# Statistics, norm and weight sums of the first batch, and the last three outputs, put on other engines in a two-layer attention kernel

## The chip, the cores and the metric

The kernel runs on one core of a Trainium2 chip. The metric is the device time of one execution in microseconds (us); less is better. PE stands for TensorE, PEld for its weight loads, DVE for VectorE, ACT for ScalarE, POOL for GpSimd and SP for SyncE, which issues most DMAs.

## The reference

The input `x` holds 8 images of 32x32 tokens with 512 channels, in fp32. Two layers follow each other. Each normalises `x` over groups of 16 channels (no scale, no shift), applies attention and adds the result to `x`:

```
x = x + proj(attention_16_heads_of_32(gn(x) @ w_qkv)) + b_proj
x = x + attention_4_heads_of_128(gn(x) @ Wq, Wk, Wv, with position logits) @ Wo
```

where `gn(v) = (v - mean) / sqrt(var + 1e-5)` over the 1024 tokens and the 16 channels of a group. The second layer's scores get two logits per pair of positions, from the queries and two small embeddings.

## The kernel before

All work is in fp32, channels on the partitions: one image is a block of 128 partitions x 4 chunks of channels x 1024 tokens. Products of 512x512 weights are formed by a seven-product scheme: the image's two halves and the weights' quarters are first combined into sums, then seven smaller products replace eight. The sums of the image ("forms", `forming`, L436) are four additions of 128x1024 on VectorE; the sums of the weights (`Matrix.add_up`, L177) are four subtractions of 128x512 a matrix, once for the whole run, stored to DRAM (L179) for the later batches.

A pass over the batches weaves three things on TensorE: the first layer's attention of batch b, what is left of batch b - 1 (projection, second layer), and the loading and projections of batch b + 1. The order of the instructions on each queue is decided when the program is built: the functions are generators that yield after each piece, `woven` and `side_by_side` pull from them in turn, and a scheduler then places the instructions. `tc.issue_after(x)` keeps an instruction behind `x` in that order.

What the change touches is the start and the end, where there is only one batch.

The start is `load_first`, then the sums of WV0, WQ0 and WK0 (value, query and key weights of the first layer), then `before_first`. `load_first` fetches the image's rows in eight DMAs on SP and ACT (L1175) and the three weights on SP (L163). TensorE turns the rows into channels, 32 blocks of 128x128 (L1193): the first 512 tokens (h = 0) into one PSUM tile of four banks, the second 512 (h = 1) into four tiles of a bank each. ScalarE copies each bank to SBUF (`x0T`, L1201), and VectorE takes the statistics of each bank (L1203). TensorE runs eight matmuls whose result is not used (L1207). VectorE aggregates (L318) and averages over groups (L329 to L354), GpSimd takes the power -1/2 (L363), VectorE normalises four chunks of 128x1024 (L367, into `xn`) and forms the sums (L436). SP stores the four chunks of `x0T` for the later residual (`put_away`, L275) and then fetches the next image in blocks (`xs`, L293).

Then come the weight sums: of WV0 two on GpSimd and two on VectorE, of WQ0 and WK0 four each on VectorE, placed behind the last form (`last_form`). `before_first` makes half of the values, queries and keys with `seven`: products x, y and z of 32 matmuls or fewer into three banks; between them VectorE adds snapshots `a` (L487) and `b` (L495) out of the bank y, and TensorE must not add the next product into y before VectorE has read it. `begun[0]` is the latest `a`.

The end is `after_last`: the output projection of the last batch, units u = 0 and u = 1, in `in_two_parts` with `five_alone` for the last five products. As each quarter of a unit's result is added to the residual (L672), `put_out` turns it in 32x32 blocks on VectorE (L1380) and sends it out in four DMAs of 64 KB, on SP and ACT in turn (L1385); each is made of pieces of 128 bytes, 32 channels of one token. Unit 1's quarters come in the order (0,0), which is sent long before the end, then (0,1), (1,1) and (1,0), the last of which waits for the last product.

Of the kernel before, what the change touches and what calls it, by code (L numbers as in the profile page):

```python
# [9 lines left out]
F32 = mybir.dt.float32  # L10
# [17 lines left out]
def quick_path(  # L28
# [123 lines left out]
    class Matrix:  # L152
# [12 lines left out]
        def add_up(self, engines, store, keep=False):  # L165

            t = self.t
            whole = t[:, : CC // 2, :].rearrange("p a (b n) -> p (a b) n", n=NB)
            sums = t[:, CC // 2 :, :].rearrange("p a (b c n) -> p (a b) c n", c=HC, n=HN)
            b11, b12, b21, b22 = [quarter(whole, i) for i in (11, 12, 21, 22)]  # L170
            for i, (x, y) in enumerate(
                [(b12, b11), (b22, sums[:, 0]), (b22, b12), (b21, sums[:, 1])]
            ):

                engine = engines[i]
                with tc.issue_after(last_form[0].ins) if engine is nc.vector else nullcontext():
                    engine.tensor_tensor(sums[:, i], x, y, op=ALU.subtract)  # L177
            d = dram.tile([P, 4, HC, HN], F32, tag="sums", name=f"ws_{self.name}", bufs=8)
            store.dma_start(d, sums)  # L179
            self.t = d  # L180
            self.kept = (whole, sums) if keep else None

        def factor(self, i):

# [138 lines left out]
    def group_norm(st, xT, name, after=None, behind=None, out=None, apart=False):  # L323

        mv = st.pop("mv")

        def averages(out, src, tag):
            total = small.tile([P, 2], F32, tag=f"total{tag}", name=f"total{tag}_{name}")
            nc.vector.tensor_reduce(  # L329
                total, src.rearrange("p (g k) -> p g k", k=GROUP_CHANNELS), axis=AX.X, op=ALU.add  # L330
            )
            nc.vector.tensor_scalar(
                out.rearrange("p (g k) -> p g k", k=GROUP_CHANNELS),
                total.unsqueeze(2).to_broadcast([P, 2, GROUP_CHANNELS]),
                1.0 / GROUP_CHANNELS,
                None,
                op0=ALU.mult,
            )

        turned = small.tile([P, 32], F32, tag="turned", name=f"turned_{name}")  # L340

        with tc.issue_after(after().ins) if after is not None else nullcontext():
            nc.vector.transpose(turned, mv)
        avg = small.tile([P, 2, 32], F32, tag="avg", name=f"avg_{name}")
        averages(avg[:, 0, :], turned, 0)

        nc.vector.tensor_sub(turned, turned, avg[:, 0, :])
        nc.vector.tensor_mul(turned, turned, turned)
        averages(avg[:, 1, :], turned, 1)
        back = small.tile([P, 2, 32], F32, tag="back", name=f"back_{name}")  # L350
        nc.vector.transpose(back.rearrange("p a c -> p (a c)"), avg.rearrange("p a c -> p (a c)"))
        mean = back[:, 0, :CC]
        var = small.tile([P, CC], F32, tag="var", name=f"var_{name}")
        nc.vector.scalar_tensor_tensor(  # L354
            var, back[:, 0, CC : 2 * CC], GN_EPS, back[:, 1, :CC], op0=ALU.add, op1=ALU.add
        )
        if apart:

            mean = small.tile([P, CC], F32, tag="mean0", name=f"mean_{name}")
            nc.vector.tensor_copy(mean, back[:, 0, :CC])  # L360
            yield 0
        rstd = small.tile([P, CC], F32, tag="rstd0" if apart else "rstd", name=f"rstd_{name}")
        nc.gpsimd.tensor_tensor(rstd, var, neg_half, op=ALU.pow)  # L363
        yield 0
        for cc in range(CC):
            with tc.issue_after(behind().ins) if behind is not None else nullcontext():
                nc.vector.tensor_scalar(  # L367
                    xT[cc] if out is None else out[cc],
                    xT[cc],
                    mean[:, cc : cc + 1],  # L370
                    rstd[:, cc : cc + 1],
                    op0=ALU.subtract,
                    op1=ALU.mult,
                )
            if cc % 2 or apart:
                yield 0
# [793 lines left out]
    def load_first(st):  # L1170

        rows = block("x_rows", [P, NT, C])
        for t in range(NT):
            queue = nc.scalar if t % 2 else nc.sync
            queue.dma_start(rows[:, t, :], xf[0, t * P : (t + 1) * P, :])  # L1175
        for m in (WV0, WQ0, WK0):
            m.fetch(nc.sync)
        x = block("x0T_0")
        xT = chunks(x)
        looks = mem.tile([P, NB], F32, tag="row", name="looks", bufs=3)  # L1180
        looks = looks[:, : CC * NH * 6].rearrange("p (c h s) -> p c h s", c=CC, s=6)
        looks = [looks[:, cc] for cc in range(CC)]
        looked, copied = [None], [None]
        for h in range(NH):
            if h == 0:
                whole = wide_tile("turned_0")
                banks = [whole[:, cc, :] for cc in range(CC)]
            else:
                banks = [bank(f"turned_1_{cc}") for cc in range(CC - 1)]
                banks.append(psum.tile([P, NB], F32, tag="acc", name="turned_1", bufs=1))  # L1190
            for t in range(NT // NH):
                for cc in range(CC):
                    nc.tensor.transpose(  # L1193
                        banks[cc][:, t * P : (t + 1) * P],
                        rows[:, h * (NT // NH) + t, cc * P : (cc + 1) * P],
                        ident,
                    )
            for cc in (0, 2, 1, 3):
                part = xT[cc][:, h * NB : (h + 1) * NB]
                with tc.issue_after(copied[0].ins) if copied[0] is not None else nullcontext():  # L1200
                    copied[0] = nc.scalar.copy(part, banks[cc])  # L1201
                with tc.issue_after(looked[0].ins) if looked[0] is not None else nullcontext():
                    looked[0] = nc.vector.bn_stats(looks[cc][:, h, :], banks[cc])  # L1203

        idle = wide_tile("idle")
        for t in range(NT):
            nc.tensor.matmul(idle[:, t % CC, :], ident, rows[:, t, :], start=True, stop=True)  # L1207
        st["mv"] = mvs[0]
        mvs.reverse()
        for cc in (0, 2, 1, 3):  # L1210
            aggregate(st, looks[cc], cc)
        st["kept"] = put_away(xT, "0_0")

        xn = block("xn0_0")
        run(group_norm(st, xT, "0_0", out=chunks(xn)))
        st["xn"] = forms(xn, "xn0_0")

# [156 lines left out]
    def put_out(b, st, xT, u):  # L1374
        def put(n, h):
            m = n * HC + u
            ot = mem.tile([P, NB], F32, tag="row", name=f"ot_{b}_{m}_{h}", bufs=3)
            late = b == B - 2
            with tc.issue_after(added[0].ins) if late else nullcontext():
                nc.vector.transpose(ot, xT[m][:, h * NB : (h + 1) * NB])  # L1380
            ot = ot.rearrange("p (t i) -> p t i", i=32)
            for a in range(P // 32):

                queue = nc.scalar if b == B - 1 and a % 2 else nc.sync
                queue.dma_start(  # L1385
                    by_blocks(of[b, h * NB : (h + 1) * NB, :], m * P + 32 * a),
                    ot[32 * a : 32 * a + 32],
                )

        def put_later(n, h):  # L1390
            st.setdefault("late", []).append(lambda: put(n, h))

        return put_later if b == B - 2 else put

    def late_output(st):

# [4 lines left out]
    def after_last(b, st):  # L1401

        x = st["ao"]
        xT = fetch(st["kept"], block(f"x2T_{b}"))
        sinks = [Onto(halves(xT, u), then=put_out(b, st, xT, u)) for u in range(2)]
        run(
            in_two_parts(
                x, WO, sinks, f"wo_{b}", behind=(None, None, None, lambda: begun[0]), in_turn=True,
                first=ends.pop(),
            )  # L1410
        )

    def woven(main, side, start, gap, places=(0,)):

# [78 lines left out]
    ends = []  # L1493
    load_first(states[0])
    WV0.add_up([nc.gpsimd] * 2 + [nc.vector] * 2, nc.gpsimd, keep=True)
    WQ0.add_up([nc.vector] * 4, nc.gpsimd, keep=True)
    fill_fold()
    stream = Stream(plan)

    def key_sums():  # L1500
        WK0.add_up([nc.vector] * 4, nc.gpsimd, keep=True)
        yield 0

    def other_sums():
        for m in (WP, WQ1, WK1, WV1, WO):
# [1 line left out]
            m.add_up([nc.gpsimd] * 4, nc.gpsimd)  # L1507
            yield 0

    run(woven(before_first(states[0]), key_sums(), 3, 1))  # L1510
    for b in range(B + 1):
        rest, total = [], 0
        s = [None] * 2 + states + [None] * 2
# [577 lines left out]
```

## Time and profile before

| What | Value |
|---|---|
| Time, median of 3 runs | 3664.14 us (3663.9 to 3664.3) |
| The profiled execution | 3663.89 us |
| Its span in the profile | 3662.1 us |
| TensorE busy | 3633.3 us (99%) |
| VectorE busy | 2557.9 us (70%) |
| ScalarE busy | 1999.3 us (55%) |
| GpSimd busy | 1298.3 us (35%) |
| Granted TensorE clock, mean | 0.999 |

The span runs from the first to the last record of the program; 1.8 us of the profiled execution's time lie outside it. A line of the timeline has the begin in us from the span's start, the duration, the engine, the line of the kernel, the operation, the tile written and those read, the shape and the count; in brackets stands how long the engine was idle before and what ended that. Equal instructions that follow each other are merged. A line by stretches has the stretch, its length, the busy time of each engine with the number of instructions, the TensorE clock, the busy share of the 16 DMA engines and their GB/s. Ends of matmuls are modelled.

### The profile page before, as it was taken

The numbers are of one execution on the slowest core, as the hardware profiler recorded it, in microseconds if no ns is written. First come the engines' busy times: TensorE is split into PE (matmuls) and PEld (weight loads), VectorE is DVE, ScalarE is ACT, GpSimd is POOL, SyncE is SP. The second block draws the span as 40 slices with busy tenths as digits, with TensorE's granted clock in tenths as the row PEclk, the third lists the DMA queues.
The fourth block names the chain that finished last, engine by engine and source line by source line (L and its number), as shares of the span: only waits on it lengthen the run. The fifth ranks groups of instructions, "written<-read, shape, count | busy, mean of one in ns | idle before, by whom it ended". The sixth has DMA issues, their size and how long they took to land.

```text
span 3662.1 us, 81197 instructions
## 1 busy us (share of the span) xinstructions
PE 3633.3 (99%) x33996; PEld 1243.4 (34%) x34002; DVE 2557.9 (70%) x2911; ACT 1999.3 (55%) x2281; POOL 1298.3 (35%) x833
## 2 busy tenths in 40 slices
PE   8999999999999999999999999999999999999998
PEld 4222244232433234332343323433234232323343
DVE  6788657786677856679566795767856678566545
ACT  2555666546654466544665446654566545656254
POOL 1343155131541316313173131822328122165254
PEclk9999999999999999999999999999999999999999
DMA  6233164342644326343363443533336133324376
GB/s 191 67 113 105 43 172 137 83 124 66 184 128 128 90 64 192 116 129 92 79 192 103 122 95 102 183 92 118 83 98 206 53 99 79 98 93 155 97 203 146
DMA packets 582069, 431.98 MB, mean 118 GB/s; under 512 B 280608, under 2 KB 472384, under 8 KB 580672
## 3 DMA queue, kind: packets, MB, share of 16 engines
q1 hardware_dynamic: 570064, 410.92, 39.9%
q0 software_dynamic: 2608, 13.70, 1.0%
q8 instruction: 270, 4.42, 0.5%
q10 hardware_dynamic: 9024, 2.10, 0.3%
q14 instruction: 103, 0.84, 0.1%
HBM read 334.30 MB, written 92.27 MB: 116 GB/s over the span
## 4 chain that ended last, share of the span: by engine, by line
PE 95%; DVE 3%; ACT 1%; issue 1%; POOL 0%; DMA 0%; SPq 0%; DVEq 0%; ACTq 0%; POOLq 0%
PE ps L791 15%; PE acc L817 13%; PE ps L1010 12%; PE acc L1024 12%; PE y_v L397 4%; PE y_q L397 4%; PE y_k L397 4%; PE z_q L397 3%; PE x_v L397 3%; PE z_v L397 3%; PE x_k L397 3%; PE x_q L397 3%; PE z_k L397 3%; PE y_wp L397 2%; PE y_wo L397 2%; PE sums L839 2%
## 5 line engine op out<-in xcount | busy, mean ns | idle before, releaser
L806 ACT ACTIVATE e_room<-ps 128x2048 f32<-128x2048 f32 x512 | 961.9, 1879 | 745.7 <-PE ps L791 725.2
L829 DVE TENSOR_TENSOR e_room<-e_room 128x2048 f32<-128x2048 f32 x448 | 1078.4, 2407 | 398.7 <-ACT e_room L806 397.0
L960 POOL TENSOR_TENSOR pos<-pos,columns 128x512 f32<-128x512 f32 x448 | 645.9, 1459 | 194.3 <-DMA pos<-pr 186.5
L791 PE MATMUL ps<-q,k 32*64 32x512 f32 x8192 | 592.5, 613 | 1.0 <-ACT e_room L806 1.0
L817 PE MATMUL acc<-e_room,v 128*32 128x512 f32 x4096 | 546.8, 604 | 0.1
L1010 PE MATMUL ps<-q,k 128*128 128x512 f32 x1024 | 530.2, 600 | 0.5 <-ACT ps L969 0.5
L1024 PE MATMUL acc<-e,v 128*128 128x512 f32 x1024 | 523.0, 593 | 0.0
L1013 ACT ACTIVATE e<-ps 128x512 f32<-128x512 f32 x512 | 305.8, 597 | 323.9 <-PE ps L1010 315.1
L1040 DVE TENSOR_TENSOR es<-es,e 128x512 f32<-128x512 f32 x384 | 277.8, 723 | 211.8 <-ACT e L1013 208.2
L772 POOL TENSOR_TENSOR q<-q,su 128x512 f32<-128x512 f32 x64 | 104.9, 1639 | 539.2 <-DVE su L768 515.4
L1024 PEld LDWEIGHTS acc<-e,v 128*128 128x128 f32 x1024 | 193.3, 190 | 247.6 <-issue 132.5
L969 ACT COPY ps<-pos 128x512 f32<-128x512 f32 x448 | 264.7, 592 | 10.4 <-PE ps L982 7.5
L1010 PEld LDWEIGHTS ps<-q,k 128*128 128x128 f32 x1024 | 187.3, 190 | 231.0 <-issue 207.2
L791 PEld LDWEIGHTS ps<-q,k 32*64 32x64 f32 x8192 | 122.9, 129 | 391.2 <-issue 212.1
L817 PEld LDWEIGHTS acc<-e_room,v 128*32 128x32 f32 x4096 | 81.4, 108 | 411.5 <-issue 363.6
L656 POOL TENSOR_TENSOR k<-b_k,p_k 128x512 f32<-128x512 f32 x32 | 50.1, 1566 | 479.1 <-ACT p_k L501 474.7
L656 POOL TENSOR_TENSOR q<-b_q,p_q 128x512 f32<-128x512 f32 x32 | 60.6, 1895 | 357.2 <-ACT p_q L501 342.7
L656 POOL TENSOR_TENSOR v<-b_v,p_v 128x512 f32<-128x512 f32 x32 | 50.6, 1582 | 258.8 <-ACT p_v L501 255.9
L889 ACT COPY pos<-pp 32x512 f32<-32x512 f32 x128 | 104.3, 815 | 29.2 <-PE pp L880 27.9
L1038 DVE TENSOR_TENSOR es<-e,e 128x512 f32<-128x512 f32 x64 | 64.9, 1014 | 70.4 <-ACT e L1013 70.2
L733 DVE STREAM_TRANSPOSE tu<-su 128x512 f32<-128x512 f32 x64 | 45.2, 706 | 82.4 <-ACT su L731 82.3
L397 PE MATMUL y_q<-f_xn,w_q 128*32 128x512 f32 x768 | 91.3, 593 | 1.3 <-DVE a_q L487 1.3
(233 smaller groups left out, 4564.5 us busy)
## 6 DMA issues: line engine op xcount, KB each, us to landing
pos<-pr SPq DMA_DIRECT2D x448, 256.0 KB, 3.3
w_qkv<-ws_qkv SPq DMA_DIRECT2D x168, 128.0 KB, 2.6
x1T<-d SPq DMA_DIRECT2D x32, 512.0 KB, 5.4
d<-x1T SPq DMA_DIRECT2D x32, 512.0 KB, 3.6
pc<-pos SPq DMA_DIRECT2D x32, 512.0 KB, 6.5
pr<-pos SPq DMA_DIRECT2D x32, 512.0 KB, 7.7
columns<-pc SPq DMA_DIRECT2D x64, 256.0 KB, 4.0
x2T<-d SPq DMA_DIRECT2D x32, 512.0 KB, 6.6
```

The costliest lines, as they stand in the source:

```text
L397: ins = nc.tensor.matmul(out[columns, :], weights[:, columns], moving, start=start, stop=stop, skip_group_check=open_sum,)
L656: nc.gpsimd.tensor_tensor(self.dst[1][1], s(b), s(p7), op=ALU.add)
L791: nc.tensor.matmul(ps[some, r, :], k[m][rows, j * P + 64 * i : j * P + 64 * i + 64], q[m][rows, h * NB : (h + 1) * NB], start=True, stop=True,
L806: exps[0] = nc.scalar.activation(e, ps, AF.Exp, scale=D0 ** -0.5)
L817: nc.tensor.matmul(acc[r * D0 : (r + 1) * D0, :], v[:, j, c0 : c0 + D0], e[:, r, :], start=(j == blocks[0]), stop=(j == blocks[-1]),)
L829: summed[0] = nc.vector.tensor_add(state["esum"], state["esum"], e)
L960: nc.gpsimd.tensor_tensor(self.rows[i], self.rows[i], self.columns[i // NT], op=ALU.add)
L969: self.copied = nc.scalar.copy(ps, rows)
L1010: scored[0] = nc.tensor.matmul(ps, k[h][:, keys], q[:, h, queries], start=False, stop=True, skip_group_check=True)
L1013: exps[0] = nc.scalar.activation(e, ps, AF.Exp, scale=1.0 / math.sqrt(D1))
L1024: nc.tensor.matmul(acc, v[:, j, h * D1 : (h + 1) * D1], e, start=(j == 0), stop=(j == NT - 1),)
L1040: added[0] = nc.vector.tensor_add(state["esum"], state["esum"], e)
```

## The change

There are five edits.

1. The statistics of the first half (h = 0) read ScalarE's copy in SBUF instead of the PSUM bank; those of the second half still read the banks.
2. In the first batch's norm, chunks 2 and 3 go to ScalarE as an Identity activation with scale rstd and bias -mean x rstd. The bias is a new 128x4 VectorE operation, kept in the unused end of the tile that holds the statistics. Chunks 0 and 1 stay on VectorE.
3. The sums of WQ0 and WK0 are no longer issued in a row behind the last form: each is placed behind the latest `a` (`begun`), and `first_sums` yields after each one, woven into `before_first` from its second piece on. WV0's sums stay.
4. In the built program this places WQ0's four sums and the first of WK0 between a_v and b_v, two of WK0 behind b_v and the last behind a_q; WK0's store on GpSimd comes behind the addition of a part of v. Nine matmuls of x_v's second product stand ahead of y_v's first, and one of x_q's inside z_v's last two.
5. The last three outputs of the last batch are kept back and turned by TensorE in four 128x128 transposes each, behind the last product; ScalarE copies the first two, VectorE the third, out of PSUM, and each goes out in one DMA of 256 KB, in pieces of 512 bytes: the first and third on SP, the second on ACT.

All other instructions stand in the same order on every queue. The blocks of SBUF that k of batch 0 and x0T of batch 1 use have changed places.

```diff
+        def add_apart(self, store):
+
+            whole, sums = self.keep()
+            b11, b12, b21, b22 = [quarter(whole, i) for i in (11, 12, 21, 22)]
+            pairs = [(b12, b11), (b22, sums[:, 0]), (b22, b12), (b21, sums[:, 1])]
+            for i in (0, 1, 2, 3):
+                with tc.issue_after(begun[0].ins):
+                    nc.vector.tensor_tensor(sums[:, i], *pairs[i], op=ALU.subtract)
+                if i == 3:
+                    d = dram.tile([P, 4, HC, HN], F32, tag="sums", name=f"ws_{self.name}", bufs=8)
+                    store.dma_start(d, sums)
+                    self.t = d
+                yield 0
...
-        for cc in range(CC):
+        if out is not None:
+
+            offset = st.pop("spare")
+            nc.vector.scalar_tensor_tensor(offset, mean, -1.0, rstd, op0=ALU.mult, op1=ALU.mult)
+            for cc in range(CC // 2, CC):
+                nc.scalar.activation(
+                    out[cc], xT[cc], AF.Identity, scale=rstd[:, cc : cc + 1], bias=offset[:, cc : cc + 1]
+                )
+        for cc in range(CC if out is None else CC // 2):
...
-                    looked[0] = nc.vector.bn_stats(looks[cc][:, h, :], banks[cc])
+
+                    looked[0] = nc.vector.bn_stats(looks[cc][:, h, :], banks[cc] if h else part)
...
-        return put_later if b == B - 2 else put
+        def put_last(n, h):
+            if (n, h) == (0, 0) or u == 0:
+                return put(n, h)
+            st.setdefault("late", []).append((n, h, xT[n * HC + u]))
+
+        return put_later if b == B - 2 else put_last if b == B - 1 else put
+
+    def last_output(b, st):
+
+        for i, (n, h, x) in enumerate(st.pop("late")):
+            m = n * HC + 1
+            name = f"last_{m}_{h}"
+            if i == 0:
+                turned = psum.tile([P, NB], F32, tag="acc", name=name, bufs=1)
+            else:
+                turned = bank(name)
+            for t in range(NB // P):
+                at = slice(t * P, (t + 1) * P)
+                nc.tensor.transpose(turned[:, at], x[:, h * NB : (h + 1) * NB][:, at], ident)
+            ot = mem.tile([P, NB], F32, tag="row", name=f"ot_{name}", bufs=3)
+            if i == 2:
+                nc.vector.tensor_copy(ot, turned)
+            else:
+                nc.scalar.copy(ot, turned)
+            queue = nc.scalar if i == 1 else nc.sync
+            queue.dma_start(
+                of[b, h * NB : (h + 1) * NB, m * P : (m + 1) * P].rearrange("(t p) c -> p t c", p=P),
+                ot.rearrange("p (t c) -> p t c", c=P),
+            )
...
-    WQ0.add_up([nc.vector] * 4, nc.gpsimd, keep=True)
     fill_fold()
     stream = Stream(plan)
 
-    def key_sums():
-        WK0.add_up([nc.vector] * 4, nc.gpsimd, keep=True)
-        yield 0
+    def first_sums():
+        for m in (WQ0, WK0):
+            yield from m.add_apart(nc.gpsimd)
...
-    run(woven(before_first(states[0]), key_sums(), 3, 1))
+    WQ0.keep()
+    run(woven(before_first(states[0]), first_sums(), 1, 1))
```

More of the change, by code (lines that the diff above doesn't have):

```diff
@@ L181, in add_up, with keep @@
             self.kept = (whole, sums) if keep else None
+        def keep(self):
+            whole = self.t[:, : CC // 2, :].rearrange("p a (b n) -> p (a b) n", n=NB)
+            sums = self.t[:, CC // 2 :, :].rearrange("p a (b c n) -> p (a b) c n", c=HC, n=HN)
+            self.kept = (whole, sums)
+            return whole, sums
+        def add_apart(self, store):
[10 more added lines that the diff above has]
+                yield 0
         def factor(self, i):
@@ L1179, in load_first @@
         xT = chunks(x)
-        looks = mem.tile([P, NB], F32, tag="row", name="looks", bufs=3)
-        looks = looks[:, : CC * NH * 6].rearrange("p (c h s) -> p c h s", c=CC, s=6)
+        room = mem.tile([P, NB], F32, tag="row", name="looks", bufs=3)
+        looks = room[:, : CC * NH * 6].rearrange("p (c h s) -> p c h s", c=CC, s=6)
+        st["spare"] = room[:, NB - CC :]
         looks = [looks[:, cc] for cc in range(CC)]
@@ L1411, in after_last @@
         )
+        last_output(b, st)
     def woven(main, side, start, gap, places=(0,)):
```

## The prediction

> **What bounds the kernel now.** I read the page first, then the busy time by stage, then the timelines of the two ends.
>
> ```profile
> span 3662.1 us, 81197 instructions
> PE 3633.3 (99%) x33996; PEld 1243.4 (34%) x34002; DVE 2557.9 (70%) x2911; ACT 1999.3 (55%) x2281; POOL 1298.3 (35%) x833
> ```
>
> TensorE is idle for 3662.1 - 3633.3 = 28.8 us in all. Where, the busy time by stage says (stretch, its length, then busy time of PE, PEld, DVE, ACT, POOL, then clock, DMA share, GB/s):
>
> ```profile
> 0.00:22.40 22.40, 14.72 (x50) 9.54 (x51) 10.67 (x29) 5.59 (x9) 6.77 (x17) 0.92 0.95 337
> 22.40:37.63 15.23, 12.88 (x226) 7.90 (x229) 12.91 (x18) 1.76 (x3) 2.99 (x4) 1.00 0.79 232
> 61.86:3609.00 3547.14, 3540.07 (x33234) 1204.02 (x33241) 2493.91 (x2801) 1976.16 (x2241) 1274.19 (x803) 1.00 0.41 117
> 3652.40:3662.10 9.70, 0.00 (x0) 0.00 (x0) 1.66 (x3) 0.00 (x0) 0.00 (x0) 0.66 0.60 87
> ```
>
> From 61.86 to 3609 TensorE is the bound (7 us idle in 3547). Ahead of 37.63 and behind 3652.4 something else is. The start (begin, duration, engine, line, operation):
>
> ```profile
> 9.76 0.59 ACT L1201 COPY x0T<-turned 128x512 f32<-128x512 f32 x1 [0.77 <-DVE looks L1203]
> 13.08 3.09 DVE L1203 BATCH_NORM_STATS2 looks<-turned 128x6 f32<-128x512 f32 x5 [0.65 <-ACT x0T L1201]
> 13.92 8.53 PE L1207 MATMUL idle<-x_rows,ident 128*128 128x512 f32 x16 [2.96 <-DVE looks L1203]
> 18.62 1.04 POOL L363 TENSOR_TENSOR rstd<-var,neg_half 128x4 f32<-128x4 f32 x1 [3.63 <-DVE var L354]
> 19.70 2.98 DVE L367 TENSOR_SCALAR xn<-x0T,back,rstd 128x1024 f32<-128x1024 f32 x4 [1.16 <-POOL rstd L363]
> 22.72 1.23 DVE L436 TENSOR_TENSOR f_xn<-xn 128x1024 f32<-128x1024 f32 x1
> 27.39 3.09 DVE L177 TENSOR_TENSOR prep_qkv<-prep_qkv 128x512 f32<-128x512 f32 x5
> 30.40 0.68 DVE L487 TENSOR_TENSOR a_v<-y_v,p_v 128x512 f32<-128x512 f32 x1
> 31.14 1.93 PE L397 MATMUL y_v<-prep_qkv,f_xn 128*32 128x256 f32 x32 [1.32 <-DVE a_v L487]
> 33.41 0.68 DVE L495 TENSOR_TENSOR b_v<-y_v,p_v 128x512 f32<-128x512 f32 x1
> ```
>
> Statistics, norm, forms, sums, a_v and b_v are one VectorE queue, and TensorE waits for it. The end:
>
> ```profile
> 3651.47 1.30 DVE L1380 STREAM_TRANSPOSE ot<-x2T 128x512 f32<-128x512 f32 x2
> 3652.22 4.61 ACTq L1385 DMA_DIRECT2D out<-ot  x6
> 3653.39 0.71 DVE L1380 STREAM_TRANSPOSE ot<-x2T 128x512 f32<-128x512 f32 x1
> ```
>
> ```profile
> 3658.00:3659.00 1.00, 0.00 (x0) 0.00 (x0) 0.00 (x0) 0.00 (x0) 0.00 (x0) 0.50 0.91 142
> 3659.00:3660.00 1.00, 0.00 (x0) 0.00 (x0) 0.00 (x0) 0.00 (x0) 0.00 (x0) 0.50 0.02 3
> ```
>
> TensorE ends at 3652.39; three turns, twelve stores of 64 KB in 128-byte pieces and 3.1 us from the last byte to the span's end follow.
>
> [...] on the one four-bank tile of the first half, copies and statistics take turns, 1.35 us a pair (8.41, 9.76, 11.11, 12.46); on the second half's separate tiles they overlap. [...] The trace has 597 ns at 512 and 1879 at 2048[...]; pointer operands it does not show. [...] The trace: TensorE stops at 10.96, its clock is 0.50 from 14 to 16. [...] (142 GB/s with 128-byte pieces at 1.0 busy share); stores of 512-byte pieces it does not show.
>
> **The change, part by part.** The orders of the two built programs differ on every queue at the start and the end alone; in between they are the same, so what is gained at 62 us stays gained where TensorE is the bound.
>
> Statistics. The first half's four read the copy in SBUF, so ScalarE no longer waits for VectorE on those banks. Copies then follow at (2.54 - 0.59)/4 = 0.49 us, faster than statistics at (3.09 - 0.68)/4 = 0.60. The eight run unbroken from 9.03: the last begins at 9.03 + 7 x 0.602 = 13.24, before at 15.49. Gain 2.25. L312's statistics out of SBUF take 1.24 for two, so the source costs no more (perhaps 0.2 less). The L275 stores of x0T go out earlier on SP; the third xs load now waits for the norm on ScalarE (20.0) instead of the aggregation (16.5), which costs nothing, since the next entry of SP's queue waits until past 34 for WQ0's sums anyway. The idle matmuls start at 11.0 without the 2.96 us gap, so at the full clock, 16 x 0.43 = 6.9 us, ending at 17.9. TensorE then waits about 1 us for xn[...].
>
> Norm. rstd ends at 19.66 - 2.25 = 17.41. Then a small offset (as var, 0.16) to 17.61, two VectorE pieces of 2.98/4 = 0.745 to 19.15, and beside them two ScalarE ones. Their cost is not in the trace: [...] high end 1.88 each, what 2048 elements take (3.7). [...] Nothing else is in ScalarE's queue until p_v (x_v ends near 20.9). The first form starts at 20.06 instead of 22.72: 2.66 in all so far.
>
> Sums. Before, from the first form to b_v's start: 33.41 - 22.72 = 10.69, and y_v's third product runs at 34.15. After, in VectorE's new order: forms 4.67 (22.72 to 27.39), two WV0 sums 1.20, a_v 0.60, five sums 3.01, b_v 0.68 and 0.05 to release: 10.21, so 30.27. Gain 3.88. Five sums, not four, still lie between a_v and b_v (WQ0's four and one of WK0), so b_v stays the last wait. TensorE alone would be there at 29.4: a_v done 26.6, a product 1.72, then 0.75 + 0.21 + 0.11 of z and x_q. That last 0.32 (one z, one x_q matmul) was done behind y_v before: gain 3.88 + 0.32 = 4.20. The nine x_v matmuls put ahead of y_v need p_v (21.6) and end at 22.6; y_v's form is ready at 22.5, and a_v is bound by VectorE at 25.9, so they cost nothing. WK0's last sum moves behind a_q (near 38), its store behind GpSimd's v addition; it lands near 43.5 by L179's 4.4, while SP reaches the load that needs it at 44: hidden, and SP has until 50.8 (next xs load) after that. GpSimd's v addition may fall on two WK0 sums and double them (L436 took 2.19 beside it near 3630, else 1.22), 1.2 us; a v and y_q have 2 us to spare.
>
> Tail, in the times of before. The three turns leave VectorE (1.30 + 0.71), so the last addition starts at 3652.47 and ends at 3653.15. TensorE turns the first two outputs behind its last product: four 128x128 take 0.65 (16 took 2.58 near 10) to 0.78 (32 took 6.24). Third group 3653.65 to 3654.4, copy 0.68, store at 3655.2; the last of twelve was issued at 3655.8. Stores are 3 x 256 KB at 3653.8, 3654.4, 3655.2. First bytes follow an issue by 0.95 (3652.21, 3653.15). At the 300 GB/s or so that the loads reach near 37, 256 KB take 0.85, so the stores hardly queue: last byte near 3657.1 instead of 3658.95. Gain 1.8. Ends: 2.5, if the last store lands 2.1 us after issue as the first small ones do, and -0.6, if bytes go no faster than now (768 KB in 4.9 us from 3654.75). ScalarE issues one store instead of six and copies two tiles (0.59 each), behind which only its flag load stands.
>
> Sum: 4.2 + 1.8 = 6.0. The profiled execution took 3663.89 (its span and 1.8 around it), 0.25 under the median 3664.14. So 3657.9 for it, 3658.1 for the median. A measurement tells about 0.2% (7.3 us) from no change; this is 0.16%.
>
> **Rivals.** A, as above: start 3.6 to 4.8, tail 1.0 to 2.4: 3657 to 3659.6. B, more comes out: [...] statistics out of SBUF 0.2 faster, tail at its upper end (0.7): 6.0 + 1.3 = 7.3, just the bound; with the aggregation's and the norm's small steps a little shorter too, 7.7 and 3656.4. [...] Against: b_v still bounds. C, it doesn't do what it says: copies and statistics still alternate (x0T is now shared), the 2.25 stay lost: 3660.4. Against: in the built program three copies carry no wait. D, slower: the new stores, 512 pieces of 512 B each at a 2 KB pitch, write far slower than read. The start's 4.2 is eaten when the last byte comes 4.2 later than 3658.95, that is 768 KB in 8.4 us, at 94 GB/s; at 80 it is 3665.5. Against: 128-byte pieces already go at 142.
>
> **How the numbers follow.** A 79%, B 13%, C 5%, D 3%. Part of A's and B's border lies at the bound: faster 0.15, same 0.82, slower 0.03. The range takes in most of B and reaches to C: 3656.3 to 3660.4.
>
> **What would show it.** Copies back to back from 8.41 and the last statistic near 13.2; the first form near 20.1; b_v near 29.6 and y_v right behind it; x_q to y_q 4.2 earlier; the last byte 3 us or so ahead of the span's end and 4.8 us behind TensorE's last product. Wrong if ScalarE's two pieces end past 21, if DMA stays busy beyond 5 us after the last product, or if idle time between 62 and 3600 leaves 7 us.

## The result and the profile after

| | Before | After |
|---|---|---|
| Time, median of 22 runs each | 3664.22 us (3663.56 to 3664.86) | 3658.64 us (3658.05 to 3659.61) |
| The profiled execution | 3663.89 us | 3658.98 us |
| Its span | 3662.1 us | 3657.1 us |

The ratio is 0.9985, with a 95% interval of 0.9979 to 0.9991. The change takes 5.6 us, 0.15%, off the time; 6.0 were forecast, 3658.1 us. It is a gain, since the interval leaves out 1, but smaller than the 0.2% (7.3 us) that the prediction took as the least that a measurement can tell.

The page of the kernel after, its span and the busy time of the engines:

```profile
span 3657.1 us, 81222 instructions
PE 3635.3 (99%) x34014; PEld 1248.8 (34%) x34014; DVE 2549.2 (70%) x2908; ACT 2002.7 (55%) x2285; POOL 1298.6 (36%) x833
```

TensorE is busy 2.0 us longer (1.5 of it the transposes) and the span is 5.0 shorter: all of the gain, and more, is idle time of TensorE. The busy time by stage of the kernel after, cut at the corresponding events:

```profile
0.00:18.90 18.90, 12.98 (x48) 8.62 (x49) 9.05 (x28) 6.11 (x10) 6.77 (x17) 1.00 0.93 326
58.50:3605.40 3546.90, 3540.74 (x33241) 1203.99 (x33241) 2487.66 (x2801) 1976.34 (x2241) 1272.00 (x801) 1.00 0.42 117
3648.80:3657.10 8.30, 1.46 (x12) 1.19 (x12) 1.38 (x2) 1.07 (x2) 0.00 (x0) 0.86 0.37 104
```

The middle is as it was (6.2 us idle against 7.1). What lies ahead of it went from 61.86 to 58.5, what lies behind TensorE's last product from 9.7 to 8.3. The timeline of the start, kernel after:

```profile
8.48 2.05 ACT L1230 COPY x0T<-turned 128x512 f32<-128x512 f32 x4 [4.55 <-PE turned L1222]
9.10 2.47 DVE L1233 BATCH_NORM_STATS2 looks<-x0T 128x6 f32<-128x512 f32 x4 [5.58 <-ACT x0T L1230]
11.49 2.47 DVE L1233 BATCH_NORM_STATS2 looks<-turned 128x6 f32<-128x512 f32 x4
12.75 2.61 POOL L177 TENSOR_TENSOR prep_qkv<-prep_qkv 128x512 f32<-128x512 f32 x2 [8.58 <-DMA prep_qkv<-in_L_conv_w_qkv]
14.79 0.60 DVE L352 TENSOR_SCALAR avg<-total 128x32 f32<-128x32 f32 x1
18.18 2.37 ACT L390 ACTIVATE xn<-x0T,looks,rstd 128x1024 f32<-128x1024 f32 x2 [5.29 <-DVE looks L388]
20.59 1.23 DVE L464 TENSOR_TENSOR f_xn<-xn 128x1024 f32<-128x1024 f32 x1 [1.06 <-ACT xn L390]
30.05 0.59 ACT L529 COPY p_v<-z_v 128x512 f32<-128x512 f32 x1 [3.40 <-PE z_v L425]
30.07 0.68 DVE L523 TENSOR_TENSOR b_v<-y_v,p_v 128x512 f32<-128x512 f32 x1
30.81 0.42 PE L425 MATMUL y_v<-prep_qkv,f_xn 128*32 128x256 f32 x3
```

The four copies follow each other without a gap and the statistics form one row, as forecast. One small step is strange: L352 takes 0.60 us where it took 0.18. ScalarE's pair takes 2.37. b_v is nearly tied with the copy of p_v. The timeline of the end, kernel after:

```profile
3648.72 1.54 PE L1441 MATMUL last<-ident,x2T 128*128 128x128 f32 x12
3650.02 1.38 SPq L1448 DMA_DIRECT2D out<-ot_last  x2
3650.30 0.69 DVE L1444 COPY ot_last<-last 128x512 f32<-128x512 f32 x1 [0.75 <-PE last L1441]
```

And its stretches of 1 us (the last two columns are the share of the DMA engines that is busy and GB/s):

```profile
3651.00:3652.00 1.00, 0.00 (x0) 0.00 (x0) 0.00 (x0) 0.00 (x0) 0.00 (x0) 1.00 1.05 295
3653.00:3654.00 1.00, 0.00 (x0) 0.00 (x0) 0.00 (x0) 0.00 (x0) 0.00 (x0) 1.00 0.76 213
3654.00:3655.00 1.00, 0.00 (x0) 0.00 (x0) 0.00 (x0) 0.00 (x0) 0.00 (x0) 0.88 0.18 51
```

The stores run at twice the rate of before (295 GB/s at a busy share of 1.05, where the kernel before had 144 to 154 at 1.03 to 1.07), end for most DMA engines at 3653.75, and then trail for another 1.3 us at a small share of the engines.

### Marks used below

Five distances, read from single instructions in each trace, tell the kernels apart: **S** from TensorE's first turn to the begin of the last statistic, **R** from there to the end of rstd, **F** from there to the first form, **Q** from there to y_v's third product, **K** from there to the first scores; and **T** from the end of the last product to the end of the span. "Faster by" is the median of the kernel before, run beside it on the same chip, less its own (us).

| Kernel | S | R | F | Q | K | T | Faster by | Interval of the ratio |
|---|---|---|---|---|---|---|---|---|
| before | 10.77 | 4.17 | 3.06 | 11.43 | 27.64 | 9.68 | | |
| after | 8.49 | 4.59 | 2.71 | 10.22 | 27.62 | 8.34 | 5.58 | 0.9979 to 0.9991 |
| after_again | 8.49 | 4.49 | 2.70 | 10.23 | 27.62 | 8.07 | 5.47 | 0.9979 to 0.9992 |
| start_only | 8.48 | 4.18 | 2.70 | 10.23 | 27.62 | 9.92 | 3.65 | 0.9984 to 0.9997 |
| tail_only | 10.77 | 4.18 | 3.05 | 11.43 | 27.64 | 8.09 | 1.56 | 0.9987 to 1.0004 |
| stats_banks | 10.76 | 4.17 | 2.71 | 11.22 | 27.63 | 8.57 | 2.55 | 0.9984 to 1.0001 |
| norm_dve | 8.48 | 4.53 | 3.06 | 10.23 | 27.61 | 8.41 | 4.78 | 0.9981 to 0.9994 |
| wv0_later | 8.56 | 4.25 | 3.78 | 11.25 | 27.64 | 8.56 | 3.38 | 0.9984 to 0.9997 |
| sums_in_a_row | 8.37 | 4.32 | 2.70 | 11.43 | 26.76 | 8.08 | 4.48 | 0.9981 to 0.9994 |
| sums_behind_b | 8.40 | 4.61 | 2.70 | 9.47 | 27.61 | 8.62 | 5.72 | 0.9978 to 0.9991 |
| two_by_pe | 8.55 | 4.46 | 2.70 | 10.23 | 27.62 | 8.75 | 4.87 | 0.9980 to 0.9993 |
| best | 8.75 | 4.18 | 2.47 | 9.46 | 27.62 | 8.07 | 5.81 | 0.9978 to 0.9991 |
| tail_128 | 8.48 | 4.42 | 2.70 | 10.23 | 27.62 | 12.01 | 1.53 | 0.9987 to 1.0004 |
| tail_512 | 8.49 | 4.38 | 2.71 | 10.23 | 27.62 | 11.22 | 2.45 | 0.9985 to 1.0002 |

An interval of 0.0006 to either side is 2.2 us. Differences between two of these kernels that are smaller rest on the marks, not on the medians.

### The profile page after: what moved, and what is told of

Same layout as the page of the kernel before. It is cut to its first block, busy times and chain, and to the rows that moved or that the text cites. A ratio compares the mean times of both kernels' runs of the same rounds, so it can differ in the third digit from the quotient of the medians.

```text
span 3657.1 us, 81222 instructions
## 1 busy us (share of the span) xinstructions
PE 3635.3 (99%) x34014; PEld 1248.8 (34%) x34014; DVE 2549.2 (70%) x2908; ACT 2002.7 (55%) x2285; POOL 1298.6 (36%) x833
## 3 DMA queue, kind: packets, MB, share of 16 engines
q8 instruction: 270, 4.42, 0.5%
## 4 chain that ended last, share of the span: by engine, by line
PE 96%; DVE 2%; ACT 1%; issue 1%; POOL 0%; DMA 0%; SPq 0%; ACTq 0%; DVEq 0%; POOLq 0%
PE ps L819 15%; PE acc L845 13%; PE ps L1038 12%; PE acc L1052 12%; PE y_v L425 4%; PE y_q L425 4%; PE y_k L425 4%; PE x_v L425 3%; PE z_q L425 3%; PE z_v L425 3%; PE x_k L425 3%; PE x_q L425 3%; PE z_k L425 3%; PE y_wp L425 2%; PE y_wo L425 2%; PE sums L867 2%
```

## Experiments

**Start and end apart.** In start_only the last outputs leave as before; tail_only is the kernel before with the new last outputs.

```diff
-        return put_later if b == B - 2 else put_last if b == B - 1 else put
+        return put_later if b == B - 2 else put
...
-        last_output(b, st)
```

> The changed kernel with its last three outputs turned and stored as before. Theory: start and end are gains of their own that add up. In the two traces the start gave 3.4 us up to the first scores and 3.6 up to the last product, so this kernel should take about 3660.6 (3.6 less than before's 3664.2). Rival: the 5.6 us between the medians lie in one place, and the profiles' split of 3.6 and 1.4 is that of two single executions; then it would be as fast as the changed kernel (3658.6) or as slow as the one before.

> The kernel before with nothing but its last three outputs turned by TensorE and stored in 512-byte pieces. Theory: 1.4 us less than before as in the profiles, up to 2.0 by the medians (5.6 less 3.6): 3662.2 to 3662.8. In its trace the last bytes should again trail behind on one DMA engine after the bulk has ended some 2.8 us after the first byte. Rival: the long thin end of the changed kernel's stores was an accident of that execution; then the last byte comes 1 us earlier and the kernel is 2.4 us or more faster.

The gains are 3.65 and 1.56, 5.2 together; the whole change has 5.5 to 5.6. Both theories held: two separate gains, and the last byte is late again, 6.04 us behind the last product. The interval of tail_only takes in 1, so its gain rests on T (8.09 instead of 9.68).

**The statistics' source.**

```diff
-                    looked[0] = nc.vector.bn_stats(looks[cc][:, h, :], banks[cc] if h else part)
+                    looked[0] = nc.vector.bn_stats(looks[cc][:, h, :], banks[cc])
```

> The changed kernel with all eight statistics out of the PSUM banks, as before. Theory: copies and statistics take turns again, the last statistic begins 2.2 us later, but the two WV0 sums on GpSimd (12.75 to 15.36) then end before the norm's small steps, so the one that took 0.60 instead of 0.18 is short again: 2.2 - 0.4 = 1.8 us slower, 3660.4. Rival (the prediction as written: GpSimd plays no part): 2.25 slower, 3660.9, and that step stays at 0.60. Second rival (the source of the statistics was not what made them alternate): no change.

S is 10.76 again, 2.27 later, and L352 takes 0.18 (R 4.17): the source is what made copies and statistics take turns. But the loss is 3.0, not 1.8. Q is 1.0 longer, which neither theory had. The stretches of this kernel around 25 us (third number of each line: PE busy; clock third from the end):

```profile
23.00:24.00 1.00, 0.00 (x0) 0.00 (x0) 0.96 (x2) 0.58 (x1) 0.00 (x0) 1.00 1.16 170
25.00:26.00 1.00, 0.92 (x20) 0.71 (x24) 1.00 (x2) 0.00 (x0) 0.00 (x0) 0.99 0.80 117
26.00:27.00 1.00, 1.00 (x16) 0.68 (x12) 1.00 (x2) 0.00 (x0) 0.00 (x0) 0.50 0.82 134
```

TensorE stood from 22.98 to 25.08, 2.10 us, and got half its clock (0.50) from 25.98 to 29.4, just as it worked on y_v. The 3.36 us for which it stood from 10.65 to 14.01 in the same trace were followed by no fall (1.00 in each stretch of 1 us from 8 to 25), so the length of the wait alone doesn't tell; what does isn't shown. In the kernel before, the clock fell at 13.39, 2.43 us after TensorE stopped, and was 0.50 up to 16.8, over idle matmuls, where it cost nothing: TensorE still waited 1.03 us for the form at 25.35.

**The norm on VectorE alone.**

```diff
-        if out is not None:
+        if False:
...
-        for cc in range(CC if out is None else CC // 2):
+        for cc in range(CC):
```

> The changed kernel with all four chunks of the norm on VectorE, none on ScalarE. Four take 2.98 (0.745 each) from rstd's end, against 0.16 for the offset and 2.36 for ScalarE's pair: theory, the first form begins 0.3 to 0.4 us later relative to rstd's end (3.0 after it instead of 2.67), and the time is 0.4 longer than the changed kernel's: 5.2 less than before. Rival: ScalarE's half is worth more because VectorE's queue is free from 19.4 on; then the first form would be 1 us or more later, and the gain against before 4.5 or less.

F is 3.06 instead of 2.70: 0.36, as the theory has it. The median is 0.7 above that of after_again, which the medians can't tell from 0.4.

**GpSimd's sums and the slow step.** Its two sums of WV0 come behind rstd.

```diff
...
+            [...]; late = {nc.vector: last_form, nc.gpsimd: rooted if self.name == "qkv2" else [None]}
...
-                with tc.issue_after(last_form[0].ins) if engine is nc.vector else nullcontext():
+                with tc.issue_after(late[engine][0].ins) if late[engine][0] is not None else nullcontext():
...
-        nc.gpsimd.tensor_tensor(rstd, var, neg_half, op=ALU.pow)
+        rooted[0] = nc.gpsimd.tensor_tensor(rstd, var, neg_half, op=ALU.pow)
```

> The changed kernel with GpSimd's two sums of WV0 placed behind rstd in GpSimd's queue instead of ahead of it; all else is the same. In four traces VectorE's first small multiplication of the norm (0.18 when alone) ends just when GpSimd's sums end (15.39 and 15.36; 14.99 and 14.95), so it seems to stand still until GpSimd is through. Theory (such an operation on VectorE waits for a GpSimd addition that is running): the small step is 0.18 again, but the two VectorE pieces of the norm now wait for one or both of the sums (1.3 each, from 17.4 on), the first form begins at 20.5 to 21.6 instead of 20.03, and the kernel is up to 1.5 us slower than the changed one. Rival (they only share bandwidth for an instant, or the slow step is chance): rstd and the first form come 0 to 0.4 earlier, and the kernel is as fast as the changed one or 0.4 faster.

The timeline of this kernel:

```profile
17.36 3.14 POOL L177 TENSOR_TENSOR prep_qkv<-prep_qkv 128x512 f32<-128x512 f32 x2
17.41 1.23 DVE L388 SCALAR_TENSOR_TENSOR looks<-back,rstd 128x4 f32<-128x4 f32 x1 [1.23 <-POOL rstd L383]
18.56 2.49 DVE L395 TENSOR_SCALAR xn<-x0T,back,rstd 128x1024 f32<-128x1024 f32 x2
```

An operation on 4 elements, 0.16 us alone, takes 1.23 beside the first addition on GpSimd, which begins 0.05 ahead of it; VectorE's pair takes 2.49 instead of 1.53; L352 is 0.18 again. F is 1.08 longer, TensorE's clock is 0.50 from 21.4 to 24.8 (Q 1.03 longer), and the time is 2.1 above after_again. The theory held; its price lacked the clock. It isn't all of VectorE: in after the statistics beside the same sums (12.75 to 15.36) keep their pace (2.47 for four at 11.49, as at 9.10). In the changed kernel the statistics end so early that L352 falls on the end of GpSimd's sums, which start when the weights land (12.13 to 12.75 in these traces). It ends with them: 15.39 and 15.36 in after, 14.99 and 14.95 in sums_in_a_row, and 0.03 to 0.04 behind them in all eight traces in which it is slow. In start_only, where they end at 14.74, and in best, where it begins late, at 15.06, it takes 0.18. So whether L352 is slow in the changed kernel hangs on when the weights land.

**The order of the sums.** In a row again, and six of eight behind b_v:

```diff
+    WQ0.add_up([nc.vector] * 4, nc.gpsimd, keep=True)
...
-        for m in (WQ0, WK0):
-            yield from m.add_apart(nc.gpsimd)
+        WK0.add_up([nc.vector] * 4, nc.gpsimd, keep=True)
+        yield 0
...
-    WQ0.keep()
-    run(woven(before_first(states[0]), first_sums(), 1, 1))
+    run(woven(before_first(states[0]), first_sums(), 3, 1))
```

```diff
-                with tc.issue_after(begun[0].ins):
+                with tc.issue_after((begun if self is WQ0 and i < 2 else half_done)[0].ins):
```

> The changed kernel with the weight sums of query and key issued in a row behind the forms, as before. From the first form to b_v's start it took 10.69 us before and 9.48 after. Theory (VectorE's queue up to b_v is what TensorE waits for): the 1.2 us come back, 3659.8. Rival: the copy of p_v, which ends at 30.64 and b_v at 30.75, is as late by itself, so the new order gained little: no more than 0.2 us lost, 3658.8.

> The changed kernel with only two of the eight sums left between a_v and b_v; the other two of WQ0 and all of WK0 come behind b_v. Theory (b_v in VectorE's queue is the last that TensorE waits for there): b_v begins as soon as y_v's second product ends, about 2.8 after a_v instead of 3.6, y_v's third product 0.8 earlier, and the time is 0.8 less than the changed kernel's, 6.4 less than before. Rival (TensorE itself is as late: its z and x_q matmuls end only 0.2 ahead of b_v, and p_v's copy follows): y_v's third product comes 0 to 0.2 earlier, or what is gained there comes back as a wait before x_q or y_q, and the time is the changed kernel's.

In a row Q is 11.43 again, 1.21 longer, as the theory has it. But K is 0.86 shorter. The timeline of this kernel shows why:

```profile
25.59 1.93 PE L425 MATMUL z_v<-prep_qkv,xn 128*32 128x256 f32 x32
27.59 0.59 ACT L529 COPY p_v<-z_v 128x512 f32<-128x512 f32 x1 [1.34 <-PE z_v L425]
30.87 0.68 DVE L523 TENSOR_TENSOR b_v<-y_v,p_v 128x512 f32<-128x512 f32 x1
31.61 1.93 PE L425 MATMUL y_v<-prep_qkv,f_xn 128*32 128x256 f32 x32 [0.17 <-DVE b_v L523]
```

Three of WQ0's sums now stand ahead of a_v, behind WV0's two. While TensorE waits for a_v, it does the whole first product of z_v (32 matmuls as the trace counts them, two for each of the program's, at 25.59; in after 18 of them). So 18 of the second product's 32 come ahead of y_v's third product, where after has one, and this work is then missing behind it. So up to the first scores the order of the sums is worth 0.35, not 1.2; the medians say 1.0, within what they can tell. Both theories were half right. With six of the sums behind b_v, Q is 9.47, 0.76 shorter, and K the same: VectorE's queue was the last wait, as the theory has it. The timeline of sums_behind_b:

```profile
28.97 0.69 DVE L523 TENSOR_TENSOR b_v<-y_v,p_v 128x512 f32<-128x512 f32 x1 [0.82 <-PE y_v L425]
29.73 1.96 PE L425 MATMUL y_v<-prep_qkv,f_xn 128*32 128x256 f32 x31
```

Here b_v waits for TensorE, so no more is to be had from the sums.

**The last outputs.** One of the three leaves ahead as before; or all three are turned by TensorE, and leave in twelve DMAs, in pieces of 128 bytes or of 512:

```diff
-            if (n, h) == (0, 0) or u == 0:
+            if n == 0 or u == 0:
...
-            if i == 2:
+            if i == 1:
...
-            queue = nc.scalar if i == 1 else nc.sync
+            queue = nc.sync if i == 1 else nc.scalar
```

```diff
+            for a in range(P // 32):
+                at = slice(m * P + 32 * a, m * P + 32 * a + 32)
+                (nc.scalar if a % 2 else nc.sync).dma_start(of[b, h * NB : (h + 1) * NB, at].rearrange("(t p) c -> p t c", p=P), ot[:, :, 32 * a : 32 * a + 32])
```

```diff
+            for t in range(NB // P):
+                at = slice(h * NB + t * P, h * NB + t * P + P)
+                (nc.scalar if t % 2 else nc.sync).dma_start(of[b, at, m * P : (m + 1) * P], ot[:, t])
```

> The changed kernel with the first of the three last outputs turned on VectorE and stored in four pieces of 64 KB as before, ahead of the last product's end; only two are turned by TensorE. Theory (the stores' bytes are the chain: 768 KB follow each other at 280 GB/s from 2.2 us behind the last product): a third of them goes out early, the last store is issued 0.2 earlier and finds the engines free, and the span behind the last product is 7.6 to 7.8 instead of 8.1 to 8.3; 0.5 us faster than the changed kernel, 6.1 less than before. Rival (the late engine that the instruction fetch holds up sets the end, and the 128-byte pieces are slow): no gain or up to 0.5 slower.

> The changed kernel with its last three outputs, turned by TensorE as there, stored in twelve DMAs of 64 KB in 128-byte pieces, SP and ScalarE in turn, as before the change. Theory (the size of the pieces makes most of the tail's gain): a DMA engine takes 14 ns for a piece of 128 bytes and 28 for one of 512, so its share of 768 KB takes 5.4 instead of 2.7 us; the last byte comes at 2.2 + 5.4 and some of the fetch, 8 to 8.8 us behind the last product instead of 6.3, and the kernel is 1.7 to 2.5 us slower than the changed one. Rival (turning on TensorE instead of VectorE is what pays): no more than 0.5 slower.

> As the last, twelve DMAs of 64 KB, but each of 128 tokens by 512 bytes: the changed kernel's bytes and pieces with the number of issues of before. Theory (pieces, not issues): within 0.4 us of the changed kernel, since six issues a queue of 0.75 us each end about 5 us behind the last product, with the last 64 KB landing at 6.2 to 6.5. Rival (the number of issues makes the gain): as slow as the kernel with 128-byte pieces, 1.7 us or more slower than the changed one.

Two_by_pe is no faster (T 8.75). 93% of its bytes have landed 4.35 us behind the last product, 0.55 earlier than in after, but the last one at 6.32, as late as ever, and 2.44 us follow it instead of 2.05. So the bulk of the bytes isn't what ends last; a few late pieces are, from one DMA engine as it seems (below). The fetch of instructions described there was long in this trace, 1.63 us instead of 1.22; without that difference the last byte would be some 0.4 earlier, so the bulk may count for a part.

The theory on the pieces fell. Its prices are those of the traces: from 3654 to 3657 of before, 1616 and 1601 packets, nearly all of 128 bytes, take 47.0% and 50.3% of 16 x 3 us, 14 and 15 ns each; from 3651 to 3653 of after, 604, nearly all of 512 bytes, take 53.2% of 16 x 2 us, 28 ns each. But TensorE's turn with the old twelve DMAs (tail_128) is 2.1 slower than start_only, which has the same pieces; 1.5 of it is the first byte, which comes 2.17 instead of 0.67 us behind the last product. Pieces of 512 bytes give back 0.8 by T (0.9 by the medians), and three stores instead of twelve another 3.0 to 3.15. These prices hold for this order of the steps; three stores with VectorE's turn weren't tried. In tail_512, 96% of the pieces land at 6.12 (after_again: 5.17), the last at 8.50 (6.02), and 2.72 instead of 2.05 us follow: 0.95 + 1.53 + 0.67. Its stretches show the first:

```profile
3651.00:3652.00 1.00, 0.00 (x0) 0.00 (x0) 0.00 (x0) 0.00 (x0) 0.00 (x0) 1.00 0.94 264
3652.00:3653.00 1.00, 0.00 (x0) 0.00 (x0) 0.00 (x0) 0.00 (x0) 0.00 (x0) 1.00 0.35 88
```

SP's fifth and ScalarE's fourth issue take 1.00 and 1.53 us instead of 0.4, and the DMA engines run dry; what these issues wait for isn't settled. The second goes with a second fetch of instructions, of 1.79 us (2.8% of 16 x 4 us), which begins 5.98 us behind the last product, amid the last stores; in after the second one begins at 6.15, just before the last byte. This is its line in tail_512 from 3653.5 to 3657.5 (transfers, MB, share of the time of 16 engines):

```profile
q8 instruction: 1, 0.02, 2.8%
```

The third lies in SP's last eight waits for stores, one for each of eight semaphores. This is the line of them in tail_512, and then in after:

```profile
L1674 SPq EVENT_SEMAPHORE  x8: 17/17/17, 3657.4 to 3658.0; - x8
```

```profile
L1674 SPq EVENT_SEMAPHORE  x8: 17/17/17, 3651.9 to 3655.4; - x8
```

With twelve stores all eight waits come behind the last landing, with three only the last one.

**The late engine, and a better kernel.** Best is sums_behind_b with three chunks of the norm on VectorE and one on ScalarE:

```diff
-            for cc in range(CC // 2, CC):
+            for cc in range(CC - 1, CC):
...
-        for cc in range(CC if out is None else CC // 2):
+        for cc in range(CC if out is None else CC - 1):
```

> The changed kernel itself, a second time, as the measure for the three others of this call, and as a third trace of its start and end. In eight traces with this tail or one like it the last byte comes 5.06 us plus the duration of the 16 KB instruction fetch (0.95 to 1.65) after the last product's end. Theory: so again here, within 0.1. Rival (chance): the last byte is 0.2 or more away from that sum. The time: 5.2 to 5.9 less than before.

> The changed kernel with two improvements that the runs point to: six of the eight weight sums behind b_v (0.76 from the first form to the first scores by the traces, 37.08 against 37.84), and three chunks of the norm on VectorE and one on ScalarE. From rstd's end that is 0.16 + 3 x 0.745 = 2.40 on VectorE and some 1.35 on ScalarE, against 2.67 with two and two: the first form 0.25 earlier. Theory: 1.0 us faster than the changed kernel of the same call. Rival (TensorE, dense from the first form on, takes back what the queue gives): 0 to 0.3 faster.

The DMA queues of after from 3651 to 3653 (packets, MB, share of the time of 16 engines) show, besides the stores on q1 and q10, one transfer of instructions, 1.22 us, 3.8% of 16 x 2 us. By the size of all such transfers in before (270 on q8, 4.42 MB) it is one of 16 KB:

```profile
q8 instruction: 1, 0.02, 3.8%
```

| | after | again | in a row | norm_dve | wv0_later | stats_banks | best | tail_only | behind b |
|---|---|---|---|---|---|---|---|---|---|
| Fetch, us | 1.22 | 0.96 | 0.96 | 1.30 | 1.45 | 1.46 | 1.05 | 1.08 | 1.65 |
| Last byte behind the last product | 6.29 | 6.02 | 6.02 | 6.36 | 6.51 | 6.52 | 6.01 | 6.04 | 6.57 |
| Difference | 5.07 | 5.06 | 5.06 | 5.06 | 5.06 | 5.06 | 4.96 | 4.96 | 4.92 |

After_again met the theory (5.06). The expectation counted eight earlier traces; two_by_pe, with other stores, gives 4.69, and two others 4.92 and 4.96. The last pieces of after come one by one, 24 ns apart, at a busy share of 0.07 to 0.09 from 3654.4 to 3654.9, as from a single engine of the 16 (0.06). The author's reading, which no trace shows, is that one engine has the fetch to do amid its share of the stores, and the end of the program waits for it. No kernel here set out to move the fetch, and the trace doesn't name the engine, so this stays a correlation, though a close one.

Best has F 2.47 and Q 9.46 and the first scores 0.97 earlier than after_again, 57.28 against 58.25: the theory's 1.0. (S and R are 8.75 and 4.18 here, but together they are within 0.05 of after_again's.) Of this 0.7 is left in the span (3655.9 against 3656.6) and 0.3 in the median (3658.21 against 3658.55), which lies within the scatter of 21 runs each. It is the fastest of all by its trace; by its times it can't be told from the changed kernel.

## Why the prediction was right, and where it was not

**Statistics** (2.25 forecast): S fell by 2.28. What had taken turns was the accesses to one tile: the copy at 9.76 waits for the statistic of 9.03, which reads another bank of the same tile (the loop takes the banks 0, 2, 1, 3). **Norm** (0.41): F fell by 0.35. ScalarE's pair took 2.37; no trace of before has an activation of 128x1024 with scale and bias read from SBUF, so the forecast's price for it was not shown. **Small steps**: the sum had them unchanged; R grew by 0.42 and 0.32 in two traces of the changed kernel and by 0.01 in start_only. This is most of what made the first form 20.59 instead of 20.06; the rest is 0.06 of the norm and 0.08 by which TensorE's first turn came later in this trace. The prediction moved VectorE's steps 2.25 earlier and did not ask what GpSimd would be doing then.

**Sums** (1.21 by order): Q fell by 1.21, but sums_in_a_row shows that the order of the sums isn't what earned most of it. Without the new order Q + K would still have fallen by 0.88, since TensorE then does more of z_v ahead while it waits; the prediction took the whole of what VectorE's queue loses as gain and didn't ask how TensorE would use the longer wait. The further **0.32** for one z and one x_q matmul done ahead came to nothing: K is 27.62 against 27.64. Matmuls of this form overlap each other: one alone takes 0.40 us (z_v at 30.69 of after), and three together 0.42 (y_v at 30.81), so one that is done ahead by itself may save little. That this is the reason was argued, not tested. That b_v stays the last wait was right (sums_behind_b), by a margin of 0.1 to p_v's copy.

**Start in all**: 3.4 in the profile of after and 3.5 in that of after_again, 3.9 in start_only, where L352 took 0.18, 4.2 forecast. **Middle**: what was gained at the first scores stayed. Behind it comes another 0.3 between 340 and 718 us (the a of the same place: 3.33 earlier at 340, 3.62 at 718, 3.63 at 3440), in start_only 0.4. Its cause is open. Best gains nothing there (4.59 at 340 and at 718), which is where 0.35 of its lead over after_again goes.

**Tail** (1.8): 1.34 and 1.61 in the two traces, 1.8 to 1.9 by the medians (5.5 less 3.65). The size is near by luck, the working isn't right. The last byte was put 4.7 us behind the last product and came at 6.0 to 6.3, so that one of the prediction's own signs of being wrong, DMA busy beyond 5 us, did come. Three stores of 0.85 each were taken to hardly queue, but their issues are 0.5 apart, so 94% of the 768 KB went in one row from 2.17 to 4.97 at 263 GB/s, and then the last pieces were late. Against that the part behind the last byte, left at 3.1, shrank from 2.82 to 2.05 (the 3.1 was misread: the last byte of before comes at 3659.24, not 3658.95). The two errors cancel but for 0.2 to 0.5. And the gain was credited to faster bytes, while fewer stores bring 3.0 of it and TensorE's turn costs 2.1.

**Clock**: forecast as no loss, with idle matmuls at the full clock and a wait of about 1 us behind them; so it came (7.03 us from 10.96, then 0.91 of waiting, at 1.00 in each stretch of after from 8 to 34). That the clock wouldn't fall was the author's estimate: stats_banks (0.50 for 3.4 us) and wv0_later (0.50 from 21.4 to 24.8), with Q 1.0 longer in both, show that it could have been a loss of 1 us. Of the rivals, C (still alternating) and D (slow pieces) fell by the first trace. B's upper ends didn't come: four statistics take 2.47 us out of SBUF as out of PSUM, and the tail had no 0.7 more.

## What to carry to other kernels

A step that is moved earlier meets what other engines do at that time: look what will run beside it (here L352 took 0.60 us instead of 0.18 beside GpSimd's sums) and how long TensorE will then stand, not only what it waited for. A queue that is shortened is worth only what TensorE couldn't do ahead meanwhile (here 0.35 of 1.21 us), so count the work that will be missing from its wait. At the end of a kernel count the stores: here three large ones instead of twelve were worth more (3.0) than the slower way of turning cost (2.1).

## What was not expected of the hardware

- An operation of VectorE on 128x4 elements took 1.23 us instead of 0.16 beside one addition on GpSimd (wv0_later), and one on 128x32 took 0.60 instead of 0.18 (after).
- In stats_banks TensorE stood for 2.1 us, and 0.9 later its clock was 0.50 for 3.4 us; 3.36 us of standing in the same trace were followed by no fall.
- Where a 16 KB fetch of instructions, of 0.96 to 1.65 us, fell amid the last stores, the last byte came 4.92 to 5.07 us plus the fetch's duration behind the last product in nine traces. That the fetch is the cause wasn't tested.
- TensorE still loses 0.8 us near 3645 of after: it waits for ScalarE's copy of p_wo, which stands behind six store issues (3639.86 to 3644.4) in ScalarE's queue. To issue these on SP alone wasn't tried.
